# Graph attention on one core: the attention stage put into a written order on all engines, with masks made one step ahead

## The chip, the cores and the metric

The kernel runs on one core of one Trainium2 chip. The metric is device time in microseconds (us) of one execution. Nine runs of the kernel before gave a median of 2029.53 us (2022.5 to 2035.93). The profile comes from one more execution, which took 2020.07 us; its trace spans 2018.3 us.

## What is computed

The program is two graph layers with a residual and a layer norm after each, on 6250 nodes, 100000 edges (sorted by target `dst`) and 128 features. The change touches only the second layer's attention:

```
z  = h @ fc_w.T ;  rh = r_h @ fc_r_w.T            # r_h: the edge features
e  = z[src] @ aw[0] + z[dst] @ aw[1] + rh @ aw[2]
e  = where(e >= 0, e, 0.01 * e)
ex = exp(e - segment_max(e, dst)[dst])
alpha = ex / segment_sum(ex, dst)[dst]            # a softmax over the edges of each target
agg = segment_sum(alpha[:, None] * (z[src] + rh), dst)
out = relu(agg + z @ loop_w)
```

The first layer (two graph convolutions) has the same pattern of fetching rows by `src` and summing them by `dst`.

## The kernel before, in words

The edges are cut into 49 chunks of 2048. A chunk's targets lie in a window of 144 nodes. Earlier stages sort a chunk's edges by source into 17 groups of 128 slots: 12 groups whose source rows are in SBUF (`hot`), and 5 groups (`far`) whose rows are fetched from DRAM by POOL's indirect DMAs.

Attention (from line 1232) needs two things for a chunk: the scores of its edges, and then the weighted sums.

The scores come in steps of a generator, `scores()`, which is worked through by `deal(count)`. The chunks are grouped in 8 batches (of 2, 5 and then 7 chunks). For a batch there are:

- `ends(c0, n)`: the target's part of the score for up to four chunks. DVE makes masks from `dk`, PE multiplies them with `a_d` (L1284), DVE reduces, SP stores `adg` in DRAM.
- `starts(c)`: the source's part, two lookup steps a chunk. DVE makes a mask `rk` (L1309) and a one-hot `ohb` (L264), with ACT's copy L1312 between; PE does 24 matmuls (L1317) into the one buffer of `ps_k`; DVE multiplies with the one-hot (`sel`, L1320) and reduces (`asr`, L1321).
- `softmax(b)`: the softmax of a batch, with scans on DVE, one exp on ACT, matmuls that hand a value to the next partition (L1347), a store of the result to DRAM (`shd`) and a read back in another layout (`al`). It leaves `ready[b]`.

The sums of a chunk are in the main loop:

- `shares`: DVE makes `ohm`, `ohg` and `put` (L264, L270), ACT makes `al2` (L1442), PE adds up over 16 matmuls (L1446), DVE reduces to `swt` (L1447), the weight of every slot.
- `pick`: 144 bf16 matmuls (L544) take the near rows from `hot`; ACT scales them by `swt` into `got` (L549).
- `edge_sums`: DVE makes the masks `mb` and `ms` (L264, L1477), PE multiplies them with the edge features `et` (L1485), ACT copies the result `sw` (L1490).
- `sum_masks`: masks by target, `wb` and `fb` on DVE, turned by ACT into `wm` (L580, L597).
- `scatter`: 36 matmuls (L606) sum the rows of the chunk before into its window, in the one buffer of `ps_w`; `add_in` (L614) adds the window to `acc2` on DVE.
- `bring`: five indirect DMAs on POOL (L560) fetch the far rows. They wait for the first matmul of the scatter behind which they are written.
- `in_place`: DVE makes `pl` (L1498), PE brings the edge sums to their window columns (L1502), ACT copies `sr` (L1504).
- `pieces`: as soon as four blocks of nodes are complete, `out_of` transposes them (L499), adds the residual, normalises and stores.

The order of the work is set in two ways. The earlier stages stand in `tc.manual_schedule()`: each engine runs its instructions in the order in which the program writes them. Attention does not: there a scheduler orders the instructions by priority and by its own estimate of when they can start, so lookups of later batches may run far ahead of where the program writes them. On the chip each engine and each DMA-issuing queue (SP's, POOL's) then runs in the order it was given.

Of the kernel before, what the change touches and what calls it, by code (L numbers as in the profile page):

```python
# [9 lines left out]
F32 = mybir.dt.float32  # L10
BF16 = mybir.dt.bfloat16
# [8 lines left out]
P = 128  # L20
# [5 lines left out]
TC = 16  # L26
# [14 lines left out]
def gnn_kernel(ctx, tc, x, src, dst, ea, ew, W1, b1, W2, b2, fcw, fcrw, attn, loopw, out):  # L41
# [446 lines left out]
    def out_of(sum_x, sum_r, b0, n, xp, pool, tag):  # L488

        some = blocks[b0 : b0 + n]  # L490
        fin = xp.tile([P, 4, D], F32, name="fin", bufs=1)
        load_some(nc.sync, fin, x1d, b0, n)
        yield
        agg = pool.tile([P, 4, D], F32, name="agg", tag=tag)
        for b, nb in some:
            of = slice(b * P, b * P + nb)
            if sum_r is not None:
                nc.tensor.matmul(agg[:nb, b - b0, :], sum_r[:, of], wfrT, start=True, stop=False)
            nc.tensor.matmul(agg[:nb, b - b0, :], sum_x[:, of], ident, start=sum_r is None, stop=True)  # L499
        for p, k in whole(some, b0):  # L500
            nc.vector.scalar_tensor_tensor(fin[:p, k, :], agg[:p, k, :], 0.0, fin[:p, k, :], op0=OP.max, op1=OP.add)
        yield
        yield from normed(fin, some, b0, xp)
        store_blocks(nc.sync, out, fin, b0, n)
# [728 lines left out]
    with tc.tile_pool(name="look", bufs=2) as lp, tc.tile_pool(name="conv3", bufs=2) as wp, \  # L1233
# [42 lines left out]
        def ends(c0, n):  # L1276

            dk = dks.pop(c0)
            nc.vector.tensor_scalar(dk[:, : n * P], dk[:, : n * P], iotap, None, op0=OP.is_equal)
            ps = ps_c.tile([P, 4, J, NK], F32, name="rec")  # L1280
            for c in range(n):
                lo = blos[c0 + c]
                for k in range(3):
                    nc.tensor.matmul(ps[:, c], dk[:, c * P : (c + 1) * P], a_d[:, k, :, lo : lo + NK], start=k == 0, stop=k == 2)  # L1284
            load_ends()
            yield
            got = lp.tile([P, 4, J, NK], F32, name="got", bufs=1)
            near = lp.tile([P, 4, J], F32, name="near", bufs=1)
            adg = lp.tile([P, 4, TC], F32, name="adg")
            one = lp.tile([P, 2, TC, J], F32, name="one", bufs=1)  # L1290
            nc.vector.tensor_tensor(got[:, :n], ps[:, :n], oh5[:, c0 : c0 + n, None, :].to_broadcast([P, n, J, NK]), op=OP.mult)
            nc.vector.tensor_reduce(near[:, :n, :], got[:, :n], AX.X, OP.add)
            for c in range(0, n, 2):
                m = min(2, n - c)
                two, some = slice(c, c + m), [P, m, TC, J]
                nc.vector.tensor_tensor(one[:, :m], iotab[:, None, None, :J].to_broadcast(some),
                                        dlb[:, c0 + c : c0 + c + m, :, None].to_broadcast(some), op=OP.is_equal)
                nc.vector.tensor_tensor(one[:, :m], one[:, :m], near[:, two, None, :].to_broadcast(some), op=OP.mult)
                nc.vector.tensor_reduce(adg[:, two], one[:, :m], AX.X, OP.add)
            nc.vector.tensor_add(adg[:, :n], dots[:, c0 : c0 + n, :], adg[:, :n])  # L1300
            nc.sync.dma_start(adgd[P + c0 * CC : P + (c0 + n) * CC].rearrange("(c p t) -> p c t", p=P, t=TC), adg[:, :n])

        def starts(c):

            for h in range(2):
                of = slice(h * NL // 2, (h + 1) * NL // 2)
                sources(2 * c + h + AHEAD)
                mk = rks.pop(2 * c + h)
                nc.vector.tensor_scalar(mk, mk, iotap, None, op0=OP.is_equal)  # L1309
                ohb = lp.tile([P, NL // 2, NBE], BF16, name="ohb")  # L1310
                blk2 = lp.tile([P, NL // 2, 2], BF16, name="blk2")
                nc.scalar.copy(blk2, twice(blks[:, c, of]))  # L1312
                equal_to(ohb, blk2, NBE)
                ps = ps_k.tile([P, NL // 2, NB], F32, name="k")
                for s in range(NL // 2):
                    for k in range(3):
                        nc.tensor.matmul(ps[:, s, :], mk[:, s * P : (s + 1) * P], adp[:, 0, k, :NB], start=k == 0, stop=k == 2)  # L1317
                yield
                sel = lp.tile([P, NL // 2, NB], F32, name="sel")
                nc.vector.tensor_mul(sel, ps, ohb[:, :, :NB])  # L1320
                nc.vector.tensor_reduce(asr[:, 1 + c * NL + of.start : 1 + c * NL + of.stop], sel, AX.X, OP.add)  # L1321
# [3 lines left out]
        def softmax(b):  # L1325

            c0, n = batches[b]
            R = n * NL + 2
            ad = lp.tile([P, P], F32, name="ad", bufs=1)
            nc.sync.dma_start(ad[:R, :], adgd[c0 * CC : c0 * CC + R * P].rearrange("(r j) -> r j", j=P))  # L1330
            ps = ps_c.tile([P, P], F32, name="rec")
            nc.tensor.transpose(ps[:R, :], asr[:, c0 * NL : c0 * NL + R], ident)
            yield
# [19 lines left out]
            def spread(of, k):  # L1353

                nc.vector.tensor_tensor(of, of, end, op=OP.mult)
                nc.vector.tensor_tensor_scan(full[:, ::-1], go[:, ::-1], of[:, ::-1], 0.0, op0=OP.mult, op1=OP.add)
                ps = moved(k, full[:, 0:1], behind)
                yield
                took(k, ps)
                nc.vector.tensor_tensor_scan(full[:, ::-1], go[:, ::-1], of[:, ::-1], sm[:, k : k + 1], op0=OP.mult, op1=OP.add)  # L1360
# [4 lines left out]
            ps = moved(0, part[:, P - 1 :], before)  # L1365
            yield
            took(0, ps)
# [7 lines left out]
            ps = moved(2, part[:, P - 1 :], before)  # L1375
            yield
            took(2, ps)
# [6 lines left out]
            nc.sync.dma_start(shd[c0 * CC : (c0 + n) * CC].rearrange("(r j) -> r j", j=P), e_[1 : R - 1, :])  # L1384
            ps = ps_c.tile([P, P], F32, name="rec")
# [3 lines left out]
            yield  # L1389
            yield  # L1390
            aw = lp.tile([P, MB * NL], F32, name="aw")
            nc.scalar.copy(aw[:, : n * NL], ps[:, 1 : R - 1])
            al3 = lp.tile([P, MB, TC, 3], BF16, name="al3")
# [10 lines left out]
        def scores():  # L1404
            yield from all_ends(0)
            for b in range(NT):
# [5 lines left out]
                next(rest)  # L1412
                yield
                yield from all_ends(b + 1)
                yield from rest
                yield


        with tc.high_priority():
            for i in range(AHEAD):  # L1420
                sources(i)
            for _ in range(2):
                load_ends()
            steps = scores()
            next(steps)
# [8 lines left out]
        def shares(c, al3, i):  # L1434
# [8 lines left out]
            spread_out(put, ohg, al2, 3)  # L1443
            ps = ps_c.tile([P, 3, GE], F32, name="rec")
            for t in range(TC):
                nc.tensor.matmul(ps, ohm[:, t, :], put[:, t, :], start=t == 0, stop=t == TC - 1)  # L1446
            nc.vector.tensor_reduce(swt[:, c, :], ps[:, :, :G].rearrange("p k g -> p g k"), AX.X, OP.add)  # L1447

# [18 lines left out]
        def edge_sums(c, aw, i):  # L1467

            k = min(NL, -(-(E - c * CC) // P))
            full = k if c < CF else crem // P  # L1470
            ets = features.pop(c)
# [5 lines left out]
            nc.vector.tensor_mul(ms, mb, aw[:, i, :, None].to_broadcast([P, NL, WS]))  # L1477
            ps = ps_r.tile([P, NL // 8, D], F32, name="r")
# [16 lines left out]
        def in_place(c, sw, sizes):  # L1495

            pl = mp.tile([P, NL // 8, WC], F32, name="pl", bufs=1)
            nc.vector.tensor_tensor(pl, iota[:, None, :WC].to_broadcast([P, NL // 8, WC]),  # L1498
                                    place[:, :, c : c + 1].to_broadcast([P, NL // 8, WC]), op=OP.is_equal)
# [9 lines left out]
        load_features(0)  # L1509
        for b, (c0, n) in enumerate(batches):  # L1510
            while b not in ready:
                deal(1)
            al3, aw = ready[b]

            more = 2 * (batches[b + 1][1] + 1) + 12 if b + 1 < NT else 0
            done, points = 0, 0
            for c in range(c0, c0 + n):
# [7 lines left out]
                shares(c, al3, c - c0)  # L1525
                beside()
                load_mask(c + 2)
                rows, _, _ = pick(c, slots_of.pop(c), hot, ps_g, wp)
                edges_ = edge_sums(c, aw, c - c0)
                load_features(c + 1)  # L1530
                beside()
                sums = sum_masks(c, wp)
                win = None
                if held is not None:
                    win = scatter(held, ps_w)
                rows += bring(c, zd, wp, 11, win and win[1])
                new = [*rows, wfrT], [*sums, (0, in_place(c, *edges_))]
                beside()
                if held is not None:
                    add_in(acc2, c - 1, win)  # L1540
                held = new
                pieces.go(lows[c], 1)
                beside()
        add_in(acc2, NC - 1, scatter(held, ps_w))
        pieces.finish()
# [179 lines left out]
```

## Time and profile before

| what | value |
|---|---|
| nine runs, median | 2029.53 us |
| the profiled execution | 2020.07 us, span 2018.3 us |
| PE busy | 1604.9 us (80%) |
| DVE busy | 1435.3 us (71%) |
| ACT busy | 1095.6 us (54%) |
| POOL busy | 884.8 us (44%) |
| mean granted TensorE clock | 0.9 |
| attention: first lookup matmul, last add into `acc2` | 1245.9 us, 1998.95 us |
| far gathers in attention (L560) | 245 of 1.04 us |
| lookup matmuls (L1317) | 2352, 98 steps of 24 |

PE is TensorE's matmuls, PEld its weight loads, DVE is VectorE, ACT ScalarE, POOL GpSimd and SP SyncE. In rows of groups and timelines, "out<-in" names the tiles; the bracket at the end of a row is the time that the engine idled before it, and what ended this. "issue" there means that the profile shows nothing that the engine waited for, and "remote" that the releaser is not known. Ends of matmuls are modelled by the profile, their starts are recorded.

### The profile page before, as it was taken

The page shows a single profiled execution, that of the slowest core. Times are in us where ns is not written, and L with a number is a line of the kernel's source. Part 1 is how long each engine was busy: PE and PEld are TensorE (multiplying, and loading weights), DVE is VectorE, ACT ScalarE, POOL GpSimd, SP SyncE. Part 2 cuts the span into 40 slices and gives each one's busy share as a digit, 9 for nine tenths or more (in the row PEclk, how much of TensorE's full clock was granted, in tenths as well). Part 3 has the DMA queues.
Part 4 walks back from the last instruction along what each step waited for, and adds up shares of the span by engine and source line. Part 5 has one row for each costly group of instructions (what it writes and reads, how often), then busy time and mean ns, then how long its engine had stood idle before and what let it go on. Part 6 is the DMA issues. An engine that isn't in the chain of part 4 may idle for free.

```text
span 2018.3 us, 78228 instructions
## 1 busy us (share of the span) xinstructions
PE 1604.9 (80%) x33818; PEld 1431.2 (71%) x33818; DVE 1435.3 (71%) x3050; ACT 1095.6 (54%) x3477; POOL 884.8 (44%) x950
## 2 busy tenths in 40 slices
PE   4986778888887868888888885688887888788885
PEld 3755767787777747777777774577777788777775
DVE  8678888878863468767776775788877677665542
ACT  3054556666666446656665664246655555546653
POOL 4033444555554366656665660023433324334432
PEclk9777999999998879989998996689999888889998
DMA  4042454555454655755665656655766666545552
GB/s 100 1 145 71 120 130 130 147 145 156 144 160 145 160 175 171 218 175 186 197 193 180 205 162 213 180 167 169 182 193 168 175 152 189 148 133 156 161 157 47
DMA packets 264240, 313.13 MB, mean 155 GB/s; under 512 B 38204, under 2 KB 193714, under 8 KB 263085
## 3 DMA queue, kind: packets, MB, share of 16 engines
q1 hardware_dynamic: 238991, 254.36, 41.2%
q0 software_dynamic: 23520, 48.22, 11.4%
q8 instruction: 268, 4.39, 0.9%
q10 hardware_dynamic: 1374, 5.45, 0.8%
q14 instruction: 87, 0.71, 0.1%
HBM read 266.75 MB, written 41.18 MB: 153 GB/s over the span
## 4 chain that ended last, share of the span: by engine, by line
PE 35%; DVE 9%; ACT 7%; issue 6%; DMA 6%; another core or an unknown queue 3%; POOL 0%; SPq 0%; DVEq 0%; ACTq 0%
PE win L606 14%; PE g L544 10%; ACT got L549 3%; PE r L1485 2%; PE k L1317 2%; DMA rk<-srow 2%; ACT wm L597 1%; PE rec L1446 1%; DVE sel L1320 1%; PE mm L467 1%; PE rec L1502 1%; PE agg L499 1%; PE mm L475 1%; DMA far<-g,sidx 1%
## 5 line engine op out<-in xcount | busy, mean ns | idle before, releaser
L560 POOL DMA_INDIRECT far<-g,sidx x490 | 573.3, 1170 | 435.9 <-PE g L544 291.3
L549 ACT ACTIVATE got<-g,swt 128x128 f32<-128x128 f32 x1764 | 484.5, 383 | 352.4 <-PE g L544 225.2
L544 PE MATMUL g<-hot,mask 128*32 128x128 bf16 x21168 | 459.5, 242 | 131.0 <-issue 114.6
L544 PEld LDWEIGHTS <-mask 128*32 128x32 bf16 x21168 | 380.7, 108 | 194.2 <-issue 175.0
L606 PE MATMUL win<-wm,got 128*128 128x144 f32 x3528 | 498.5, 297 | 10.4 <-issue 9.0
L560 POOL DMA_INDIRECT far<-zd,sidx x245 | 255.7, 1044 | 530.9 <-PE win L606 431.2
L606 PEld LDWEIGHTS win<-wm,got 128*128 128x128 f32 x3528 | 462.6, 196 | 29.1 <-issue 22.5
L597 ACT ACTIVATE wm<-fb,swt 128x64 f32<-128x64 bf16 (+1 forms) x735 | 197.0, 373 | 51.6 <-DVE swt L1447 45.3
L580 ACT CAST wm<-wb 128x864 f32<-128x864 bf16 x196 | 176.4, 942 | 55.0 <-PE rec L1502 14.8
L606 PE MATMUL win<-wm,far 128*128 128x64 f32 (+1 forms) x1470 | 183.3, 270 | 14.2 <-DMA far<-g,sidx 10.6
L606 PEld LDWEIGHTS win<-wm,far 128*128 128x128 f32 x1470 | 179.2, 192 | 15.4 <-issue 13.7
L614 DVE TENSOR_TENSOR acc<-acc,win 128x144 f32 x147 | 44.4, 302 | 167.3 <-remote 41.0
L1317 PE MATMUL k<-adp,rk 128*128 128x49 bf16 x2352 | 92.2, 194 | 45.5 <-DVE sel L1320 23.5
L264 DVE TENSOR_TENSOR wb<-iota,sdst 128x1728 bf16<-128x1728 bf16 x98 | 103.0, 1051 | 34.7 <-issue 21.9
L1317 PEld LDWEIGHTS <-rk 128*128 128x128 bf16 x2352 | 84.1, 103 | 57.2 <-issue 48.2
L264 DVE TENSOR_TENSOR ohm<-iotab,pm 128x2048 bf16<-128x2048 bf16 x98 | 119.0, 1214 | 1.2 <-PE rec L890 1.2
L582 DVE TENSOR_TENSOR wm<-iota,sdst 128x1728 f32<-128x1728 f32 x49 | 95.7, 1953 | 3.6 <-DMA g<-rows 3.6
L1012 DVE TENSOR_REDUCE dots<-et 128x12 f32<-128x1536 f32 (+1 forms) x49 | 85.9, 1753 | 1.7
L1011 DVE TENSOR_TENSOR et<-et,ar_row 128x1536 f32<-128x1536 f32 (+1 forms) x49 | 85.7, 1748 | 0.0
L357 POOL TENSOR_TENSOR hot<-low,hot 128x512 bf16<-128x512 f32 x24 | 34.4, 1445 | 116.4 <-ACT hot L356 105.6
L1320 DVE TENSOR_TENSOR sel<-k,ohb 128x392 f32<-128x392 f32 x98 | 55.1, 562 | 27.8 <-remote 16.2
L825 DVE TENSOR_REDUCE rank<-r 128x16 f32<-128x768 f32 x49 | 46.8, 954 | 36.8 <-PE r L818 36.7
(398 smaller groups left out, 2231.3 us busy)
## 6 DMA issues: line engine op xcount, KB each, us to landing
et<-in_edge_attr_dram SPq DMA_DIRECT2D x97, 512.0 KB
mask<-masks SPq DMA_DIRECT2D x98, 384.0 KB
et<-in_edge_attr_dram SPq DMA_DIRECT2D x48, 768.0 KB
rk<-srow SPq DMA_DIRECT2D x98, 256.0 KB
mask<-srd SPq DMA_DIRECT2D x49, 384.0 KB
masks<-mask SPq DMA_DIRECT2D x49, 384.0 KB
ee<-in_edge_attr_dram SPq DMA_DIRECT2D x48, 256.0 KB
dr<-dinvd SPq DMA_DIRECT2D x46, 256.0 KB
```

What stands on the lines that cost most here:

```text
L264: nc.vector.tensor_tensor(out.rearrange("p t (h d) -> p t h d", d=2), row[:, None].to_broadcast(some), of[:, :, None, :].to_broadcast(some ...
L544: picked = nc.tensor.matmul(ps[32 * q : 32 * q + 32, g, :], mask[:, (g0 + g) * P + 32 * q : (g0 + g) * P + 32 * q + 32], hot[:, 4 * (g0 + ...
L549: nc.scalar.activation(got[:, g, :], ps[:, g, :], AF.Copy, scale=swt[:, c, g0 + g : g0 + g + 1])
L560: brought = nc.gpsimd.indirect_dma_start(out=got, out_offset=None, in_=table[:, :], in_offset=bass.IndirectOffsetOnAxis(ap=sidx[:, c, g : ...
L580: nc.scalar.copy(wm[:, n0 : n0 + half], wb[:, n0 : n0 + half])
L582: nc.vector.tensor_tensor(wm[:, :NEAR].rearrange("p (g w) -> p g w", w=WC), iota[:, None, 1 : WC + 1].to_broadcast([P, GP, WC]), sdst[:, c ...
L597: nc.scalar.activation(m, b, AF.Copy, scale=swt[:, c, GP + g : GP + g + 1])
L606: done = nc.tensor.matmul(ps[:, n0 : n0 + m.shape[-1]], row, m, start=g == 0, stop=g == len(rows) - 1)
L1011: nc.vector.tensor_mul(part, part, ar_row[:p, None, None, :].to_broadcast([p, *part.shape[1:]]))
L1012: nc.vector.tensor_reduce(dots[:p, c : c + m, ts], part, AX.X, OP.add)
L1317: nc.tensor.matmul(ps[:, s, :], mk[:, s * P : (s + 1) * P], adp[:, 0, k, :NB], start=k == 0, stop=k == 2)
L1320: nc.vector.tensor_mul(sel, ps, ohb[:, :, :NB])
```

## The change

- The whole main loop of attention, with the first shares, stands in `tc.manual_schedule()`: a written order for every engine. The first `starts` are no longer at high priority.
- `starts` makes its masks one step ahead (`look_ahead`) and reduces the step before (`look_back`) just ahead of its own matmuls.
- In `softmax` and `ends`, `yield` stands ahead of the matmuls instead of behind them, so that a matmul's input is made in the step before.
- `shares` is split. `share_masks` of the next chunk are made in the middle of a chunk, `share_sums` of the next chunk stand at its end.
- `edge_sums` and `in_place` lose their masks to `edge_masks`, at the head of the chunk, with `sum_masks` behind it.
- The gathers wait for the last matmul of `share_sums` of this chunk (`behind_`), no longer for the first matmul of the scatter.
- The edge sums come behind the scatter, the pick behind `in_place`; before, both came ahead of the scatter.
- `steps_for(b)` counts the steps of a batch anew: 27 for most. The ends of batch 1 come behind the softmax of batch 0.
- `got` has 3 buffers instead of 4, `fin` 2 instead of 1.

```diff
@@ starts
+        def look_ahead(i):
+            if i < 2 * NC:
+                mk = rks.pop(i)
+                nc.vector.tensor_scalar(mk, mk, iotap, None, op0=OP.is_equal)
...
+                nc.scalar.copy(blk2, twice(blks[:, i // 2, i % 2 * NL // 2 : (i % 2 + 1) * NL // 2]))
+                equal_to(ohb, blk2, NBE)
+                hits[i] = mk, ohb
+        def look_back():
+            for i, ps, ohb in looked:
+                sel = lp.tile([P, NL // 2, NB], F32, name="sel")
+                nc.vector.tensor_mul(sel, ps, ohb[:, :, :NB])
+                nc.vector.tensor_reduce(asr[:, 1 + i * NL // 2 : 1 + (i + 1) * NL // 2], sel, AX.X, OP.add)
+            looked.clear()
+        def starts(c):
+            for i in (2 * c, 2 * c + 1):
+                sources(i + AHEAD)
+                look_back()
+                mk, ohb = hits.pop(i)
                 ps = ps_k.tile([P, NL // 2, NB], F32, name="k")
                 for s in range(NL // 2):
                     for k in range(3):
                         nc.tensor.matmul(ps[:, s, :], mk[:, s * P : (s + 1) * P], adp[:, 0, k, :NB], start=k == 0, stop=k == 2)
+                looked.append((i, ps, ohb))
+                look_ahead(i + 1)
                 yield
@@ softmax (three places alike)
-            ps = moved(0, part[:, P - 1 :], before)
-            yield
-            took(0, ps)
+            yield
+            took(0, moved(0, part[:, P - 1 :], before))
@@ steps of a batch
-            more = 2 * (batches[b + 1][1] + 1) + 12 if b + 1 < NT else 0
+            return 2 * (c1 + 1 - c0) + 9 + 2 * (fours_(b + 1) + (b == 1) * fours_(1))
@@ main loop
+        with tc.manual_schedule():
+            load_features(0)
+            shared = share_of(0)
+            behind_ = share_sums(0, *shared)
+            for c in range(NC):
...
-                shares(c, al3, c - c0)
+                load_mask(c + 2)
+                load_features(c + 1)
+                ms, pl = edge_masks(c, ready[b][1], c - c0)
+                sums = sum_masks(c, wp)
                 beside()
-                load_mask(c + 2)
-                rows, _, _ = pick(c, slots_of.pop(c), hot, ps_g, wp)
-                edges_ = edge_sums(c, aw, c - c0)
-                load_features(c + 1)
-                beside()
-                sums = sum_masks(c, wp)
-                win = None
+                far = bring(c, zd, wp, 11, behind_)
                 if held is not None:
                     win = scatter(held, ps_w)
-                rows += bring(c, zd, wp, 11, win and win[1])
-                new = [*rows, wfrT], [*sums, (0, in_place(c, *edges_))]
+                edges_ = edge_sums(c, ms)
+                if c + 1 < NC:
+                    shared = share_of(c + 1)
                 beside()
+                sr = in_place(pl, *edges_)
+                rows, _, _ = pick(c, slots_of.pop(c), hot, ps_g, wp, 3)
                 if held is not None:
                     add_in(acc2, c - 1, win)
-                held = new
+                beside()
                 pieces.go(lows[c], 1)
                 beside()
+                if c + 1 < NC:
+                    behind_ = share_sums(c + 1, *shared)
+                held = [*rows, *far, wfrT], [*sums, (0, sr)]
```

`beside()` deals the steps of the next batch at four points of a chunk, spread over all chunks of a batch but the last: with 27 steps and 24 points, the first 14 (the lookups) fall on the first three chunks, and the ends and the softmax on the next three. `share_of(c)` deals on until the batch of chunk c is ready, and then makes its share masks.

## The prediction, made before the changed kernel was built

> **What bounds the kernel now.** I read the busy time by stretch first, because the change touches one stage only: attention, from about 1244 us to 1999 us of the span of 2018.3 us. Columns: stretch and length, then busy us (instructions) of PE, PEld, DVE, ACT and POOL, the granted clock, DMA share, GB/s.
>
> ```profile
> 1244.00:1292.00 48.00, 25.11 (x491) 21.36 (x490) 40.91 (x124) 11.08 (x35) 4.86 (x5) 0.54 0.65 194
> ...
> 1300.00:1793.00 493.00, 408.69 (x9569) 377.35 (x9568) 373.27 (x996) 266.65 (x874) 167.05 (x155) 0.90 0.62 169
> 1793.00:1999.00 206.00, 172.17 (x3792) 158.11 (x3792) 93.38 (x236) 123.46 (x390) 78.96 (x81) 0.92 0.51 135
> ```
>
> PE is busy 83% in both long stretches, DVE 76% and then 45%. No engine is full, so the order decides. The second stretch holds 32 chunks (32 copies of `sr`) and the scoring of all later batches: 15.4 us a chunk. In the third there is no scoring left, and the copies of `sr` come every 12 us.
>
> Next I read the timeline of one chunk without scoring (start, length, engine, line, operation).
>
> ```profile
> 1843.76 3.21 PE L606 MATMUL win<-wm,got 128*128 128x144 f32 x24
> 1844.55 0.94 POOL L560 DMA_INDIRECT far<-zd,sidx  x1 [5.87 <-PE win L606]
> 1847.87 0.46 PE L606 MATMUL win<-sr,wfrT 128*128 128x144 f32 x2
> 1848.17 0.65 PE L1502 MATMUL rec<-pl,sw 128*128 128x144 f32 x4
> 1848.66 0.59 PE L1446 MATMUL rec<-put,ohm 128*128 128x54 bf16 x16
> 1849.54 0.94 POOL L560 DMA_INDIRECT far<-zd,sidx  x1 [0.30 <-issue]
> 1850.18 0.30 PE L544 MATMUL g<-hot,mask 128*32 128x128 bf16 x4 [0.66 <-issue]
> 1851.62 2.04 PE L544 MATMUL g<-hot,mask 128*32 128x128 bf16 x130 [0.50 <-issue]
> 1851.64 0.28 ACT L1504 COPY sr<-rec 128x144 f32<-128x144 f32 x1 [1.88 <-remote]
> ```
>
> The scatter (L606) ends at 1848.3 and L1502 at 1848.8, yet the `sr` copy that needs L1502 starts at 1851.64, 2.8 us later and 1.2 us after the last gather (1849.54 + 0.94). PE only trickles meanwhile. So something about the five gathers holds all engines back, until about 1.1 us after the last. Last I read what such a standstill does to the clock:
>
> ```profile
> 1730.00:1731.00 1.00, 0.00 (x0) 0.00 (x0) 0.00 (x0) 0.00 (x0) 0.88 (x1) 1.00 0.98 298
> 1731.00:1732.00 1.00, 0.00 (x0) 0.00 (x0) 0.00 (x0) 0.00 (x0) 0.00 (x0) 1.00 0.44 118
> ...
> 1734.00:1735.00 1.00, 1.00 (x50) 1.00 (x44) 1.00 (x2) 1.00 (x1) 0.00 (x0) 0.50 0.06 16
> 1735.00:1736.00 1.00, 0.92 (x34) 0.65 (x26) 1.00 (x4) 0.99 (x5) 0.00 (x0) 0.50 0.00 0
> ```
>
> After 3 us without PE work the clock is 0.50 for about 3.1 us (1733.8 to 1736.9).
>
> **The change, chunk by chunk.** The arithmetic stays; what changes is the order, now the written one on every engine. I walk a chunk from T, the end of the share sums of this chunk on PE.
>
> Durations (means of the stage by line): DVE `swt` 0.21 (L1447), `mb` 0.42, `ms` 0.69, `pl` 0.46, `wb` 1.05, `fb` 0.32; a lookup step `sel` 0.56, `asr` 0.56, `rk` 0.49, `ohb` 0.36, sum 1.97; `ohm` 1.21, `ohg` 0.30, `put` 0.60, add 0.30. PE, from timelines at clock 1.0: lookup 1.0 (24 matmuls), scatter 4.57, edge sums 1.1, in-place 0.65, pick 2.19, shares 0.59. ACT `sw` 0.37, `al2` 0.27.
>
> *Chunk with four lookup steps.* The first `beside` stands ahead of the scatter. Its lookup matmuls need the one buffer of `ps_k`, which DVE frees with `sel`. On DVE `sel` is queued behind `swt` (which waits for the share sums, so for T), `mb`, `ms`, `pl`, `wb`, `fb`: 3.15 + 0.56, about 3.6 with signals, and PE, scatter included, waits behind it. This wait is new; before, PE waited 14.8 us in all for `sel` from 1300 to 1990. Then lookup 1.0, scatter 4.57, edge sums 1.1: T+10.3. The masks made ahead meet the second wait: `put` needs `al2`, which ACT runs behind `sw`, which needs the edge sums: T+11.1. DVE then does `put` and the second `sel`: T+12.3, and PE has waited 2.0. Lookup, in-place, pick, lookup: T+17.1; the fourth step waits for its `sel`, 0.6; lookup and shares: 19.3 us. A further step adds 2.0 (DVE's 1.97).
>
> *Chunk without steps.* Shares, scatter, edge sums, `sw` with signals 0.5, in-place, pick: 0.59 + 4.57 + 1.1 + 0.5 + 0.65 + 2.19 = 9.6. The gathers are let go at T instead of at the scatter's first matmul, the same place within 0.8 us, last about 6.3 us (five at 1.25), and by the row above signals come 1.1 us later still, at T+7.7: `sw` waits from T+5.7, up to 2.0. The edge sums, moved behind the scatter, cover 1.1 of this, and nothing shows whether they run free. Bounds 9.6 and 11.6; I take 11.05, nearer to the row of the standstill, and 0.35 for the final blocks' matmuls (17.1 us of L499 over 49): 11.4, against some 12 now.
>
> *Chunk with softmax and ends steps* (4.5 steps, PE 0.27 to 0.55 each, inputs made a step earlier): 11.4 + 1.3 = 12.7. ACT's and DVE's other work stays under this (DVE 5.6 a chunk, ACT 8.4) and costs nothing; it would if DVE fell behind. On SP, the read of `al` stands behind the store of `shd`: 1742.1 to 1750.9 now, 8.8 us with two chunk loads possibly queued behind it. They are needed a chunk later, so I take 0, bound 3 a batch. The masks and `et` loads move to the head of the chunk: 0, since they have a whole chunk. `yield` moved ahead of the transposes takes waits off PE: 0 to -0.5 each, inside the 12.7.
>
> *Sum.* Each batch of seven deals 27 steps over six chunks, 14 lookups first: 3 x 19.3 + 2 x 2.0 + 3 x 12.7 + 11.4 = 111.4. Five of these, the last seven chunks without steps (79.8), the final scatter and add (4.9): 642. Before, the same from the share sums of chunk 7 (1403.4) to the last add (1999.25): 596. **+46.**
>
> Batch 1's chunks (2 to 6) deal 27 steps over four: 2 x (19.3 + 6.0) + 2 x 13.3 + 11.4 = 88.6. Chunk 0 deals 27 steps in its four points, with no scatter as cover: 10 lookups 19.7, 12 chunks of ends at 0.73 DVE us 8.8 to 10, the softmax chain 12 (scans 0.42 to 0.48, reciprocal 0.95, table load 1.28), own DVE work 5.5, store and read of the shares 0 to 8.8: 47 to 56, I take 50. With chunk 1: 150 against 111.2 (1292.2 to 1403.4). **+39.** Ahead of it, DVE is busy 40.9 of 48 us, much of it batch 1's lookups that now come later; but the chain there is two DMAs (8.3 and 2.0) and the softmax: **-2** (0 to -8).
>
> Half clock: 17 chunks have the 3.6 us wait; 3.1 us at 0.50 loses 1.55. A standstill of 2.3 us (1861.6) was not followed by it, one of 3 us was: 0 to 26, I take **+13**. The second `fin` buffer spares the last block its load (1999.3 to 2003.6): **-3.**
>
> 46 + 39 - 2 + 13 - 3 = +93. The profiled execution took 2020.07 (span 2018.3 plus 1.8), which makes 2113; the runs' median is 2029.53, which makes 2122. I say **2118**. Its own range: every chunk at 9.6 and no clock loss, 2058; every wait full, 2172.
>
> [...]
>
> **Rivals.** *Faster: the DVE queue runs ahead of PE, and only its work counts.* A lookup chunk then costs DVE's 5.6 + 4 x 1.97 = 13.4, the others 11.3 and 10. Batch 88, the rest accordingly: 595.9 becomes 517, the first seven 130: about 1962. For it: DVE is only 76% busy, and PE's waits for `sel` were small. Against: `swt` ties DVE to T in every chunk. It decides from a lookup chunk of 13.8 us downward, where the sum is zero.
>
> *Slower still: lookups inside the gathers.* The first lookup's matmuls (T+3.6) fall between the gathers; if they stand until T+7.7 as L544 did at 1850, each of 17 chunks loses 3.1: 2171. For it: that row. Against: the scatter ran at its usual pace beside gathers.
>
> *No difference.* The old scheduler may already have had this order; then 2029. Against: in the timeline PE runs lookups between picks, which the new order does not.
>
> **Chances.** Forecast 0.56, gathers 0.18, faster 0.22, no difference (within 0.3%, about what a measurement here can tell) 0.03; 0.01 of a small slowdown. Slower 0.75, same 0.03, faster 0.22. The range goes from 1998, which leaves out the larger part of the faster case, to 2175.
>
> **What would show it.** Right: PE idle ahead of L1317 for DVE `sel`, some 17 times 3 to 4 us; DVE idle ahead of `put` for ACT `al2`; a clock at 0.50 after it; lookup chunks of 19 to 21 us beside 11 to 13 for the others; chunk 0 near 50 us. Wrong: lookup chunks under 14 us, or `sel` starting before T+1. Chunks without steps under 10 us would say that the gathers no longer hold PE.

## The result, and the profile after

The changed kernel is slower: 2253.92 us median (2236.72 to 2263.11, 20 runs) against 2027.35 us (62 runs) for the kernel before, a ratio of 1.1177 with a 95% interval of 1.115 to 1.1205. The forecast was 2118, with a range up to 2175: the direction was right, and the loss is 2.4 times the one worked out (+226 instead of +93). The profiled execution spans 2255.5 us.

The page's first part, after:

```profile
span 2255.5 us, 78157 instructions
...
PE 1653.2 (73%) x33818; PEld 1483.5 (66%) x33818; DVE 1474.5 (65%) x3050; ACT 1095.1 (49%) x3477; POOL 891.6 (40%) x950
```

Each engine runs as many instructions as before, but its share of the span fell. So most of the time went into waiting. Busy time by stretch, for the attention stage of before and then of after (columns as in the prediction: stretch and length, PE, PEld, DVE, ACT, POOL, granted clock, DMA share, GB/s):

```profile
1240.00:2018.00 778.00, 615.75 (x13958) 564.09 (x13957) 516.78 (x1391) 409.75 (x1327) 255.66 (x245) 0.87 0.58 158
```

```profile
1240.00:2255.00 1015.00, 667.22 (x14070) 617.97 (x14069) 558.20 (x1404) 407.45 (x1332) 265.25 (x245) 0.78 0.45 122
```

The stage is 237 us longer, which is the whole difference of the two spans. PE stands idle 348 us in it instead of 162 (1015 - 667 and 778 - 616), and is busy 51 us more with the matmuls of the same stage, at a clock of 0.78 instead of 0.87. So 186 us of the loss are time in which PE waits, and 51 are longer work of PE, which goes with the slower clock.

Three stretches after: the first seven chunks, the chunks beside which the later batches are scored, and the last chunks, without scoring:

```profile
1300.00:1460.00 160.00, 101.02 (x2022) 93.73 (x2021) 98.67 (x244) 46.81 (x165) 33.52 (x30) 0.73 0.41 113
1460.00:2104.00 644.00, 442.42 (x9510) 412.78 (x9514) 361.57 (x888) 271.09 (x887) 178.90 (x165) 0.80 0.47 128
2104.00:2230.00 126.00, 99.76 (x2254) 91.60 (x2243) 55.52 (x134) 74.64 (x238) 47.58 (x45) 0.89 0.48 125
```

In the second, PE is busy 69%, where the stretch with scoring had 83% before. What it waits for is in the view of waits (engine, what it was to run, what released it: us, times, longest). Before, PE's only large wait with a name was that for `sel`:

```profile
PE k L1317 <- DVE sel L1320: 23.5, 29, 3.3
```

After, over the stage, the largest of PE, DVE and ACT and the next of PE's:

```profile
...
PE k L1334 <- DVE sel L1321: 162.6, 71, 8.6
DVE put L270 <- ACT al L1463: 161.1, 44, 7.6
ACT wm L580 <- DVE wb L264: 158.6, 38, 8.0
ACT sw L1523 <- PE r L1518: 156.9, 28, 9.8
...
DVE ohb L264 <- ACT blk L1313: 80.7, 32, 4.6
...
PE rec L1532 <- ACT sw L1523: 50.5, 29, 3.4
```

Read them as a ring: PE waits for DVE (`sel`), DVE for ACT (`al`, `blk`), ACT for PE (`r`) and for DVE (`wb`). No engine is the bound; each stands behind an instruction that another has not reached.

One lookup chunk shows how. PE's share sums of this chunk end at 1491.61 (start, length, engine, line, operation; in brackets the idle time ahead and what ended it):

```profile
1488.91 0.28 ACT L1313 COPY blk<-blks 128x16 bf16<-128x16 bf16 x1
1489.23 0.37 DVE L264 TENSOR_TENSOR ohb<-iotab,blk 128x400 bf16<-128x400 bf16 x1 [3.88 <-ACT blk L1313]
...
1495.40 1.18 PE L1334 MATMUL k<-adp,rk 128*128 128x49 bf16 x24 [3.79 <-DVE sel L1321]
...
1496.41 4.96 PE L606 MATMUL win<-wm,got 128*128 128x144 f32 x24
...
1504.38 0.61 DVE L270 TENSOR_TENSOR put<-ohg,al 128x864 bf16<-128x864 bf16 x1 [4.94 <-ACT al L1463]
...
1505.52 0.78 PE L1334 MATMUL k<-adp,rk 128*128 128x49 bf16 x24 [1.78 <-DVE sel L1321]
...
1506.80 3.82 PE L544 MATMUL g<-hot,mask 128*32 128x128 bf16 x144
```

The two waits of PE that the prediction named are there in place and size: 3.79 us for `sel` behind the head masks (forecast 3.6), and 1.78 us behind `put`, which waits for ACT's `al2` (shown as `al`; forecast 2.0). The scatter behind the first runs slowly (4.96 us for its first 24 matmuls at a granted clock of 0.63; 3.21 at 1.00 in the chunk of before), which the prediction had priced. It had not seen that the pick behind the second does so too (3.82 us at a granted clock of 0.55, instead of 2.19), nor that ACT's copy `blk2` (`blk`), 0.28 us long, stands behind the `got` activations, so that DVE idles 3.88 us for it. This chunk took 22.4 us between share sums; the two other lookup chunks of its batch took 26.8 and 25.1.

In the first lookup chunk of a batch the wait for `sel` itself is longer, because DVE's `ohb` stands ahead of `sel`, and needs `blk`, which ACT runs behind the casts and scalings of the chunk's head. Here T is 1464.81:

```profile
1470.84 1.29 ACT L597 ACTIVATE wm<-fb,swt 128x64 f32<-128x64 bf16 x5
1472.04 0.29 ACT L1313 COPY blk<-blks 128x16 bf16<-128x16 bf16 x2
1472.26 0.37 DVE L264 TENSOR_TENSOR ohb<-iotab,blk 128x400 bf16<-128x400 bf16 x1 [2.45 <-ACT blk L1313]
...
1473.15 1.16 PE L1334 MATMUL k<-adp,rk 128*128 128x49 bf16 x24 [7.73 <-DVE sel L1321]
```

A chunk with softmax and ends steps, 1548.9 to 1566.4:

```profile
1547.64 1.18 PE L1532 MATMUL rec<-pl,sw 128*128 128x144 f32 x4 [2.12 <-ACT sw L1523]
...
1552.54 0.23 DVE L1291 TENSOR_TENSOR got<-rec,oh 128x72 f32<-128x72 f32 x1 [3.67 <-PE rec L1285]
...
1557.03 0.29 DVE L1279 TENSOR_SCALAR dk<-dk,iotap 128x384 bf16<-128x384 bf16 x1
...
1557.38 0.41 PE L1285 MATMUL rec<-a_d,dk 128*128 128x18 bf16 x9 [4.43 <-DVE dk L1279]
1557.64 0.44 PE L1350 MATMUL rec<-ident,asr 128*114 128x128 f32 x1
1557.88 4.88 PE L606 MATMUL win<-wm,got 128*128 128x144 f32 x24
```

The input `dk` of the next step is written ahead of its matmul, but on DVE it stands behind the reductions of the step before, which waited 3.67 us for PE, and behind a finished block's statistics. PE waits 4.43 us, and the next scatter takes 4.88 us for its first 24 matmuls, at a granted clock of 0.63. From share sums to share sums, the 15 lookup chunks of the five batches of seven took 20.0 to 27.7 us, 24.5 on average (forecast 19.3 to 21.3, 20.6 on average), the 20 other chunks beside scoring 12.7 to 19.0, 15.2 on average (forecast 12.4), and the six behind them 13.2 on average (forecast 11.4). Chunk 0 took 50.3 us (forecast 50).

Of these last chunks one is shown, with T at 2136.14 and its last gather from 2141.70 to 2142.65:

```profile
2143.75 0.37 ACT L1523 COPY sw<-r 128x256 f32<-128x256 f32 x1 [1.84 <-remote]
...
2144.18 0.76 PE L1532 MATMUL rec<-pl,sw 128*128 128x144 f32 x4 [2.64 <-ACT sw L1523]
...
2144.86 3.80 PE L544 MATMUL g<-hot,mask 128*32 128x128 bf16 x144
```

PE waits 2.64 us for `sw`, and the pick behind it takes 3.80 us at a granted clock of 0.55, instead of 2.19.

### The profile page after: what moved, and what is told of

It reads as the page before. It is cut to its first block, busy times and chain, and to the rows that moved or that the text cites. A ratio compares the mean times of both kernels' runs of the same rounds, so it can differ in the third digit from the quotient of the medians.

```text
span 2255.5 us, 78157 instructions
## 1 busy us (share of the span) xinstructions
PE 1653.2 (73%) x33818; PEld 1483.5 (66%) x33818; DVE 1474.5 (65%) x3050; ACT 1095.1 (49%) x3477; POOL 891.6 (40%) x950
## 4 chain that ended last, share of the span: by engine, by line
PE 33%; DVE 14%; ACT 12%; issue 5%; DMA 3%; another core or an unknown queue 1%; POOL 0%; SPq 0%; DVEq 0%; ACTq 0%; POOLq 0%
PE win L606 14%; PE g L544 10%; ACT got L549 5%; PE k L1334 2%; ACT wm L597 2%; ACT wm L580 2%; PE rec L1532 2%; DVE wb L264 1%; DVE sel L1321 1%; PE r L1518 1%; DVE ms L1500 1%; PE mm L467 1%; DMA al<-shd 1%; DMA shd<-e 1%
## 5 line engine op out<-in xcount | busy, mean ns | idle before, releaser
L560 POOL DMA_INDIRECT far<-zd,sidx x245 | 265.3, 1083 | 742.4 <-PE rec L1471 608.1
L606 PE MATMUL win<-wm,got 128*128 128x144 f32 x3528 | 538.3, 313 | 9.3 <-issue 7.8
L606 PEld LDWEIGHTS win<-wm,got 128*128 128x128 f32 x3528 | 505.8, 212 | 24.1 <-issue 17.3
L544 PE MATMUL g<-hot,mask 128*32 128x128 bf16 x21168 | 439.3, 245 | 97.8 <-issue 90.5
L580 ACT CAST wm<-wb 128x864 f32<-128x864 bf16 x196 | 171.3, 935 | 212.7 <-DVE wb L264 159.0
L1334 PE MATMUL k<-adp,rk 128*128 128x49 bf16 x2352 | 95.9, 201 | 178.3 <-DVE sel L1321 162.6
L606 PE MATMUL win<-wm,far 128*128 128x64 f32 (+1 forms) x1470 | 182.6, 270 | 13.2 <-DMA far<-g,sidx 10.2
L606 PEld LDWEIGHTS win<-wm,far 128*128 128x128 f32 x1470 | 178.8, 192 | 14.6 <-issue 14.2
L270 DVE TENSOR_TENSOR put<-ohg,al 128x864 bf16<-128x864 bf16 x49 | 29.8, 609 | 161.6 <-ACT al L1463 161.1
L1523 ACT COPY sw<-r 128x256 f32<-128x256 f32 (+1 forms) x49 | 17.9, 366 | 172.1 <-PE r L1518 156.9
L264 DVE TENSOR_TENSOR ohb<-iotab,blk 128x400 bf16<-128x400 bf16 x98 | 35.6, 363 | 90.3 <-ACT blk L1313 80.7
```

The source lines that it names most:

```text
L264: nc.vector.tensor_tensor(out.rearrange("p t (h d) -> p t h d", d=2), row[:, None].to_broadcast(some), of[:, :, None, :].to_broadcast(some ...
L544: picked = nc.tensor.matmul(ps[32 * q : 32 * q + 32, g, :], mask[:, (g0 + g) * P + 32 * q : (g0 + g) * P + 32 * q + 32], hot[:, 4 * (g0 + ...
L560: brought = nc.gpsimd.indirect_dma_start(out=got, out_offset=None, in_=table[:, :], in_offset=bass.IndirectOffsetOnAxis(ap=sidx[:, c, g : ...
L580: nc.scalar.copy(wm[:, n0 : n0 + half], wb[:, n0 : n0 + half])
L606: done = nc.tensor.matmul(ps[:, n0 : n0 + m.shape[-1]], row, m, start=g == 0, stop=g == len(rows) - 1)
```

## The experiments

Theories: **W**, the waits of the written order and the slow clock behind them; **G**, the gathers' new place; **L**, the lookups packed into three of seven chunks in an order that can't run ahead. Ratios are against the kernel before on the same chip, with 95% intervals. They were run in five groups on five chips. On four of these the kernel before takes 1834 to 1847 us, and the changed kernel's loss is larger there (e5); on the fifth it takes 2068, near the chip of the prediction (2027).

### Who orders the instructions

e1 lets the scheduler order the changed loop, instruction for instruction the same program (it also moved some instructions of earlier stages; attention starts at 1157 us there, in e5 at 1153):

```diff
-        with tc.manual_schedule():
+        with ExitStack():
```

> The changed kernel with the written order of attention's main loop given up again: a scheduler orders the same instructions, everything else of the change stays, the gathers behind the share sums too. Theory W (the written order makes engines wait in turn: PE for sel behind the masks at the head of the chunk, DVE for small copies behind ACT's long queue, and the half clock after that): 2020 to 2080 us. Theory G (the gathers' new place costs the time): stays above 2180. Theory L (the lookups are packed into three of seven chunks and no longer run far ahead): near before as well, since a scheduler may spread them.

1.0283 (1.0212 to 1.0354). Repeated as e18:

> The changed loop ordered by the scheduler once more (1.0283 where before took 1834 us). Where before takes near 2050 us, the changed kernel's loss was 11.8 per cent instead of 15.5, so the scheduled loop should stand at 0.99 to 1.03 there if the standstills behind the gathers are what separates the two places; at 1.02 to 1.035 if not.

1.0305 (1.0243 to 1.0366); before took 1847 us there, so the question about the slower chips wasn't answered. In e18's trace PE waits 39.1 us for `sel`. e5 is the changed kernel itself on such a chip:

> The changed kernel itself, unchanged, so that the others of this call are compared with it on one chip; a chip on which the kernel before takes 1834 us was met in the runs so far, against 2027. If the loss is the same work in a worse order, its ratio to the kernel before stays near 1.118; by theory W, whose waits are fixed lengths on DVE and ACT that do not depend on the chip's DMA, the loss in us stays near 226 and the ratio is 1.11 to 1.13.

1.1553 (1.1472 to 1.1634), a loss of 288 us, where 226 and a ratio of 1.11 to 1.13 had been expected. So of 15.5 points some 12.5 are the written order; 3 remain when the scheduler orders the same program. G, which had the changed kernel stay above 2180 us, fails as the main cause; W and L are not told apart by this, since a scheduler may spread the lookups.

### One wait at a time

e2 moves the first `beside()` of a chunk, with its lookup, from ahead of the scatter to behind the edge sums:

```diff
-                beside()
                 far = bring(c, zd, wp, 11, behind_)
...
                 edges_ = edge_sums(c, ms)
+                beside()
```

> The first beside of a chunk moved behind the scatter and the edge sums; nothing else. Theory W: PE's wait for sel at this place goes (3.8 us in some 20 chunks) and part of the half clock with it: 60 to 110 us less than the changed kernel, 2145 to 2195. Theory L: the lookups are still packed, the wait comes back elsewhere, under 20 us less: above 2230.

1.1133 (1.1041 to 1.1225), as W expected: 4.2 points below e5 are some 77 us. e3 makes the three small copies (`blk2`, `al2`, `rel2`) on DVE, so that DVE doesn't wait for ACT:

```diff
-            nc.scalar.copy(al2, twice(al3[:, i]))
+            nc.vector.tensor_copy(al2, twice(al3[:, i]))
```

> The three small copies al2, blk2 and rel2 made by DVE instead of ACT; the order stays. Theory W: DVE's waits ahead of put (161 us), ohb (81 us) and mb (13 us) go; PE meets them at the second and the fourth beside, so 40 to 90 us less: 2165 to 2215. Theory L: DVE gets more work in the packed chunks, no gain or slower: 2245 to 2275.

1.1025 (1.0951 to 1.1099), 5.3 points below e5 or some 97 us, a little more than W expected. DVE's large waits for `al` and `blk` (155.4 and 91.1 us in e5) are gone, and PE's for `sel` fell from 174.7 us in e5 to 106.0. e8 gives the lookups a second PSUM bank, taken from the picks (`ps_k3` 2 buffers, `ps_g3` 2 instead of 3):

> The changed kernel with two PSUM buffers for the lookup sums (ps_k) and two instead of three for the pick (ps_g); the order stays. A lookup's matmuls then need not wait for sel of the step before. Theory W: PE's waits for sel (213 us in the changed kernel's profile) fall under 60; the pick's third group waits for ACT, about 0.7 us a chunk, 35 us back: ratio to the kernel before 1.05 to 1.10. Theory L: PE waits elsewhere, ratio within 0.01 of the changed kernel's.

1.0985 (1.0909 to 1.1061), as W expected, though PE now waits 77.3 us for `rk`. Each of the three is worth 4 to 6 points. e4 gives PE work in the first wait instead: 32 unread matmuls ahead of the first lookup in the 17 lookup chunks.

> The changed kernel with 32 matmuls added on PE, whose result nobody reads, ahead of the first beside in the chunks with lookups, so that PE works while it would wait for sel. If the half clock has a price of its own, the scatter behind it runs at full clock and the time falls by 20 to 50 us: 2205 to 2235. If the standstill alone costs, the time stays or grows by up to 15 us.

1.1498 (1.1425 to 1.1571). Its matmuls are busy 37.2 us, and PE from 1122 us on 681.7 us at a granted clock of 0.83, against 678.0 at 0.77 in e5: by the author's estimate some 33 us of the slow clock's cost were gone (678.0 - 681.7 + 37.2). All of it would be 1.8 points; the ratio fell by 0.5, with an interval that overlaps e5's. So hardly all of that time lay on the path, and it isn't shown that any did; the picks behind the other waits are not tested by this.

### Together

e6 is e2 and e3, e9 adds e8's second bank. e7 is e6 with the masks of the next chunk (`mb`, `ms`, `pl`, `wb`, `fb`, ACT's casts) made behind `add_in`, so that only five ACT scalings stand at the head of a chunk. e14 is e7 with the second bank.

> The two edits that helped most alone, together: the first beside behind the edge sums, and al2, blk2 and rel2 made by DVE. Theory W: the waits are different ones, so the gains add up in the main: ratio to the kernel before 1.06 to 1.095. Theory L: the packed lookups keep a floor, ratio above 1.10.

1.0813 (1.0721 to 1.0906), inside W's range, but the two gains would add up to 1.06.

> As the run with both edits, and all masks of a chunk (mb, ms, pl, wb, fb, with ACT's casts) made in the chunk before, behind its add; only ACT's five scalings by swt stay at the head. Then nothing but the share reduction stands on DVE between the share sums and the lookups, and ACT is free for sw. Theory W: the in-place matmuls no longer wait for sw (some 1.5 us in each of 49 chunks) and DVE's head work lies beside the pick: ratio 1.00 to 1.05. Theory L: no more than 0.01 below the run with both edits.

1.0906 (1.0835 to 1.0977): a miss, no gain over e6. PE's waits for `sel` went from 88.3 us in e6 to 104.9.

> All three edits that gained alone in the written order, put together: first stretch of lookups behind the edge sums (1.1133 of before alone), the three small ACT copies on VectorE (1.1025), two PSUM banks for the looked-up rows k, one taken from the picks (1.0985); the changed kernel itself stands at 1.1553 and the first two together at 1.0813. Theory W (the loss is the waits of the written order): in the trace of those two together PE still waits 45 us for sel in the four batches from 1362 to 1812, of 105 us in which it stands; the second bank takes most of that, about 70 us less over all batches, so 1.035 to 1.05. Theory L (what is left is that lookups lie in three of seven chunks and no engine runs ahead): 1.07 to 1.08, the waits move on to DVE's other products (rk, ohb, part).

1.0725 (1.0645 to 1.0805). PE's largest waits in its attention stage:

```profile
PE k L1334 <- DVE rk L1310: 46.1, 40, 4.5
PE rec L1532 <- ACT sw L1523: 40.2, 27, 3.5
PE rec L1364 <- DVE part L1380: 24.3, 7, 3.8
```

The wait for `sel` is gone and one for `rk`, the next thing in DVE's queue, stands in its place. Both the number and this move are what L expected; W's 1.035 to 1.05 did not come.

> The three edits at once (1.0725) and the masks of the next chunk made behind the adding in, so that five ACT scalings are all that is left at the head of a chunk (with one bank for k this brought 1.0813 to 1.0906). In the trace of the three at once PE stands 25 us for sw, 16 for rk, 21 for part and full of the softmax in the four batches from 1362 to 1800. Theory W: with two banks the sel waits that ate the gain are gone, sw's shrink to about 9, so 1.05 to 1.06. Theory L (a floor that no single wait sets): 1.07 to 1.08.

1.0625 (1.0567 to 1.0683) on the chip with 2068 us, where none of the others of this part ran, so it can't be set beside 1.0725. In its trace the wait for `rk` is 71.1 us and for `sw` 37.1. Both theories' numbers go by runs on the faster chips, so it rules out neither; `sw` did not shrink as W had it.

### The start of the first batch

e15 is e9, e16 is e14, with the written order beginning at the eighth chunk (the scheduler also moved some instructions of earlier stages):

```diff
-        with tc.manual_schedule():
+        with ExitStack() as order:
...
+                if c == batches[1][0]:
+                    order.enter_context(tc.manual_schedule())
```

> The three edits at once, but the written order begins only with the eighth chunk; the shares and sums of the first seven are ordered by the scheduler. By the traces the three at once lose 47 us up to the eighth chunk against the scheduled loop, of 93 in all. If the start in the written order is a cost of its own, the ratio falls from 1.0725 to 1.045 to 1.05; if the start is given back later, it stays at 1.07.

1.0407 (1.035 to 1.0464), below both numbers, but on the chip with 2068 us, where e9 did not run, so it can't be set beside 1.0725 either.

> All four edits and the first seven chunks ordered by the scheduler. Theory W: 1.02 to 1.035, what the scheduler gives for the whole loop (1.029). Theory L: 1.045 to 1.05, no better than with the three edits and the same start.

1.0581 (1.0516 to 1.0647). Against e14 on the same chip the start gained 0.4 points, within the intervals: the copy of `sr` of chunk 7 comes 13 us earlier (1469 instead of 1482), and 7 us are left at the end (span 2185.0 instead of 2192.2). By this pair the start is no large cost of its own. e16 against e15, on the same chip too, says that the masks made ahead cost 1.7 points there.

### The gathers

e10 puts the gathers back behind the scatter's first matmul in the written order, e11 in e1, e12 adds the second bank to e11. e17 is the kernel before with only the gathers let go by the shares.

```diff
-                far = bring(c, zd, wp, 11, behind_)
                 if held is not None:
                     win = scatter(held, ps_w)
+                far = bring(c, zd, wp, 11, win[1] if held is not None else behind_)
```

> The changed kernel, still in the written order, with the gathers given out again behind the first matmul of the scatter, as in the kernel before, instead of behind the shares' sums. Theory G (the new place of the gathers costs): from 1.1553 to about 1.12 or less. Theory W: 1.14 to 1.17, no clear change, or a little slower, since the gathers then start about 5 us later in the chunk.

1.1544 (1.1464 to 1.1624), as e5.

> The changed loop ordered by the scheduler (1.0283 of before) and the gathers given out behind the scatter's first matmul as before. If the rest of 2.8 per cent is the gathers' new place (theory G in its small form): 1.00 to 1.01. If it is the other source order, the look-ahead or the changed places of the softmax's steps: 1.02 to 1.035.

1.029 (1.0205 to 1.0376), as e1.

> The run before with two PSUM banks for k and two instead of three for the picks. In the scheduled trace PE waits only 12.5 us for sel in the four batches from 1326 to 1716, where the written order had 45 and more, so at most 1 to 1.5 per cent is to be had: 0.99 to 1.01 if the gathers were the rest, 1.01 to 1.03 if not. That the picks lack their third bank may take it back.

1.0338 (1.0256 to 1.0419): the second bank gives nothing where the scheduler orders the lookups.

> The kernel before with one part of the change alone: the five gathers of a chunk are let go by the last matmul of that chunk's shares instead of the first matmul of the scatter; its order is the scheduler's as before. In the attention stage of before, VectorE and ScalarE stand 49 and 39 us with a late signal that no instruction explains, which ends about 1 us after the last gather; in the changed kernel it is 0.4 and 16 us on the same chip, and nothing in the faster runs, whatever the kernel. If the new place of the gathers takes these standstills away (theory G with the other sign): 0.97 to 0.99 where such standstills occur (before near 2050 us), 0.995 to 1.005 where they don't (before near 1840). If the scheduler's order brings the same signals behind the gathers anyway: 1.00 in both.

0.9998 (0.9952 to 1.0043). The gathers' place costs nothing and gains nothing on these chips; G is refuted there, and the 3 points of e1 are not the gathers. All four ran where the kernel before takes 1837 to 1847 us; on the slower chips, where the late releases of the last section occur, it wasn't tried.

### The kernel before once more

> The kernel before, unchanged, for its trace on this chip (1834 to 1845 us by its times). It gives the account stage by stage that the other chip's trace can't: if it is shorter than the trace of the three edits at once (span 1961.4) by 40 to 50 us up to the eighth chunk and by about as much after it, the rest of the loss is half the first batch's start in the written order and half the chunks; if all of it lies after the eighth chunk, the start is no part of it.

One run of 2047.05 us, on a slower chip again, so the account by stage was made with e17, whose time equals that of before. From the first lookup matmul to the `sr` copy of chunk 7, e9 takes 51 us longer than e17 (205.0 against 153.7), from there to the last copy 71 us (585.0 against 513.6), and behind it 6: the loss that is left in e9 is spread over the stage. Attention from its first lookup matmul to the end, in e17 and then in e5, the changed kernel on such a chip:

```profile
1155.00:1846.00 691.00, 563.00 (x13945) 524.10 (x13944) 513.33 (x1383) 402.81 (x1319) 281.16 (x245) 0.92 0.66 177
```

```profile
1153.00:2141.00 988.00, 662.42 (x14037) 616.53 (x14034) 553.54 (x1387) 400.45 (x1313) 263.95 (x245) 0.78 0.47 124
```

From the first lookup to the end of the span, the scheduled kernel takes 691 us on the faster chip against 772 on the prediction's (1245.9 to 2018.3), the written one 988 against 1002 (1253.7 to 2255.5). So the faster chips help the scheduled order by some 80 us in this stage and the written one by some 13, which is why the loss is larger there.

No version of the changed kernel beats the kernel before.

## Why the prediction failed

Direction and mechanism were right: the written order makes PE wait for `sel` behind the head masks, DVE for `al2`, and the clock falls behind it (0.63 in the scatter and 0.55 in the pick of the first chunk shown). The sizes fell short:

- **Half clock**, +13 with a bound of 26: priced for one scatter in each of 17 chunks, while PE's busy time in the stage grew by 51 us. The slow clock also followed the shorter waits. Five of the picks of chunks 42 to 47 took 3.1 to 3.8 us instead of 2.19, and their chunks 13.1 to 14.2 us; the one whose pick took 2.19 us took 11.5, near the forecast 11.4. The granted clock was 0.55 to 0.68 in the five and 1.00 in the one. The limit had been taken from a row at 1861.6, read as 2.3 us of standstill that half clock didn't follow:

```profile
1861.60:1863.90 2.30, 0.49 (x2) 0.32 (x3) 0.48 (x2) 0.38 (x3) 0.88 (x1) 1.00 0.26 53
```

But PE was busy 0.49 us of it, and its longest gap there was 1.61 us; 1.8 us were followed by half clock (last section). How much of the 51 us lay on the path is open: by e4, hardly all of what followed the first wait.

- **"ACT's and DVE's other work stays under this ... and costs nothing; it would if DVE fell behind."** This is the step that failed. Each engine's sum of work was compared with the chunk, and the queue's order was not walked. ACT's `blk2`, `al2` and `sw` stand behind 3.2 us of `got`, 1.7 us of casts and 1.3 us of scalings. So DVE waited 161.1 us for `al` and 80.7 for `blk`, and in four of the five batches of seven PE's first wait of 3.6 us was one of 6.2 to 8.6. e3, which takes three copies of 0.2 to 0.3 us off ACT, gains some 97 us (1.1553 to 1.1025, on two chips of the same speed); the forecast had 2.0 us for `al2` in each of 17 chunks, 34 us in all.
- **"Inputs made a step earlier"**, 12.7 us for chunks with softmax and ends: earlier in the program isn't earlier in time when DVE stands at an instruction that waits for PE. The chunk shown waited 4.43 us for `dk`; over the stage `dk` and the softmax's `part` and `full` cost PE 52 us (19.7, 13.2, 11.2 and 8.0). About half of it, 27 us (10.0, 9.4, 5.3 and 1.9), lies behind chunk 0, where it was forecast as none.
- **The sum**, cut like the forecast's: from the share sums of chunk 7 to the last add 768.7 us (1464.81 to 2233.51) against 596 before, +173 where +46 and the clock's 13 stood. The 15 lookup chunks together took some 57 us more than forecast, the 20 others beside scoring as much again, and the last seven with the end 13. Up to chunk 7's share sums +61 (1403.4 to 1464.8) where 39 - 2 stood: not in chunk 0, but above all in batch 1's five chunks (112.0 us, forecast 88.6). Behind the last add +3 (22.0 against 19.0) where -3 stood. 173 + 61 + 3 = 237.
- **Signals behind the gathers**, T+7.7 in plain chunks: right in place. In the last seven chunks `sw` starts 7.55 to 7.81 us behind T and PE waits 2.2 to 2.8 us for it (forecast up to 2.0). In four of them the release is late and without a name; in the other three ACT's own scalings happen to end just there, which the forecast had not worked out. Over the stage seven `sw` copies have such a release, 12.6 us in all. In e14, on the slower chip and with ACT free earlier, the wait is longer:

```profile
2113.39 1.08 PE L1522 MATMUL r<-et,ms 128*32 128x128 f32 x32
...
2115.47 0.94 POOL L560 DMA_INDIRECT far<-zd,sidx  x1 [0.30 <-issue]
2117.43 0.37 ACT L1527 COPY sw<-r 128x256 f32<-128x256 f32 x1 [5.17 <-remote]
2117.43 0.69 DVE L1504 TENSOR_TENSOR ms<-mb,aw 128x512 f32<-128x512 bf16 x1 [3.07 <-remote]
```

The edge sums end at 2114.47, and both engines that wait for them start at the same moment, 2117.43, 1.0 us after the last gather. On the faster chips no such release occurs (last section).

- **Rivals.** DVE running ahead needed lookup chunks under 13.8 us; they took 20 to 28. Lookups held up inside the gathers: in the chunk shown the first one ran at 1495.40, between gathers, as soon as `sel` was done.

What stays open: the 3 points that remain under the scheduler (not the gathers, by e11 and e17), and how the 4 points between e9 and e1 divide among `rk`, `sw`, the softmax's steps and the packing of the lookups (L). W's estimates held for single edits and promised too much for the three together, where L's number came, so L is not ruled out. What is shown is that the written order costs some 12.5 of 15.5 points on the faster chips, and that the waits pass into each other: gains of 4.2, 5.3 and 5.7 points alone made 8.3 together, and PE's wait moved on to the next entry of DVE's queue.

## What to carry to other kernels

When a written order replaces a scheduler's, walk every engine's queue entry by entry, the small copies first: a 0.2 us copy behind 3 us of work for another purpose holds up whoever needs it (here DVE, 161.1 us for `al` and 80.7 for `blk`), and with three engines in a ring such a wait can come back on the next, as PE's 162.6 us for `sel` did here. A sum of busy times under the length of a chunk does not show that an engine is free when it is needed. One wait taken away can uncover the next, as 46.1 us for `rk` in e9, so judge a written order by all of them at once, or let the scheduler order the part with uneven work.

## What the chip showed that was not expected

**Chips differ by a tenth, and in one behaviour.** Late releases without a name ("remote"), which end about 1 us after a gather, make up 49 us of idle time on DVE and 27 on ACT in the attention stage of before on the prediction's chip (e17's expectation has 39 for ACT; the rows of the stage add up to 27), 55 and 27 on that of e13. In the experiments where before takes 1834 to 1847 us there are none in the whole program, whatever the kernel. In the last seven chunks of e7 the copies of `sr` are 9.6 to 14.3 us apart, in e14, which differs by a PSUM bank for the lookups and ran on the slower chip, 13.5 to 15.3. That these standstills are the difference between the chips is argued, not shown; the stages ahead of attention also take 91 us less on a faster chip (first lookup at 1155.0 us in e17, 1245.9 in before). On the faster chips ACT has no "remote" wait in any trace here; in e14 it had 14 for `sw`, 56.8 us in all. What held ACT there, the traces don't say.

**A standstill of 1.8 us was followed by half clock.** The changed kernel's windows around the second wait shown above:

```profile
1502.40:1503.70 1.30, 1.30 (x35) 0.96 (x35) 0.00 (x0) 0.00 (x0) 0.00 (x0) 1.00 0.98 354
1503.70:1505.50 1.80, 0.04 (x4) 0.07 (x1) 1.08 (x2) 0.65 (x3) 0.00 (x0) 1.00 0.18 68
1505.50:1506.50 1.00, 0.98 (x27) 0.98 (x27) 1.00 (x3) 0.00 (x0) 0.00 (x0) 1.00 0.02 6
1506.50:1507.50 1.00, 1.00 (x33) 0.85 (x34) 0.96 (x4) 0.28 (x1) 0.00 (x0) 0.68 0.10 33
1507.50:1508.50 1.00, 1.00 (x50) 1.00 (x44) 0.91 (x2) 0.20 (x1) 0.00 (x0) 0.50 0.60 170
```

The clock falls to 0.50 at about 1506.9, 1.4 us after PE had begun to work again (1505.52), just as the pick begins.
